# Transfers of two images at a time, edges cleared one by one and two filtered pairs in the second convolution of an attention and quantised-convolution kernel

## The chip, the core and the metric

The kernel runs on one core of a Trainium2 chip. The core has five engines that work side by side, each through its own instructions in order: TensorE (PE in the profile, its weight loads PEld), VectorE (DVE), ScalarE (ACT), GpSimd (POOL) and SyncE (SP), which here only issues transfers (DMAs). The transfers are carried out by 16 DMA engines. SBUF, the memory next to the engines, has 128 partitions; DRAM holds the inputs, the output and two intermediate arrays. The metric is the device time of one execution in microseconds (us), the median of several runs.

## What is computed

An input of 16 images with 128 channels of 32 x 32 pixels goes through two layers. The first is attention with four heads over the 1024 pixels of each image, with a residual; the second is two 3 x 3 convolutions on 4-bit activations with 4-bit weights, each followed by a batch norm over all images, with a second residual:

```python
x = out + x                                  # layer 0: attention, its output projection, residual
identity = x
out = act_quant(x)                           # clip to 0..1, round to 15 levels
out = conv3x3(out, weight_quant(w1))
out = batchnorm(out, gamma1, beta1)          # mean and variance over images and pixels
out = act_quant(out)
out = conv3x3(out, weight_quant(w2))
out = batchnorm(out, gamma2, beta2)
return out + identity
```

## The kernel before

A first phase, some 1900 of the 2013 us, does the attention and, image by image, the first convolution. It leaves two arrays in DRAM: `x1d`, the 16 x 128 x 1024 array that is the second residual (`identity`), and `y1d`, the first convolution's output for 15 of the 16 images. The last image's part of this is the end of the phase (`normalise_group`, lines 880 to 890, with `quantize` at 253 to 266, and `first_conv` at 1002).

The change lies in the last phase, lines 1149 to 1342. It does the second convolution. The images are taken in eight pairs (p = 0 to 7, images 2p and 2p + 1), and the 128 output channels in two halves (`COLS`, "part" 0 and 1). One convolution of one pair for one half fills 128 partitions of a PSUM tile: 64 channels of the first image in the upper 64 partitions, 64 of the second in the lower ones (`HALVES`). So the phase runs over all eight pairs for part 0, and then over all eight for part 1:

- Four transfers (line 1179) bring `y1d` back, 2, 3, 4 and 6 images at a time, with the channels on the partitions. They are issued by SP.
- Each image has a padded tile of 34 x 34 pixels in bf16 (`pads2`), whose edges are zero. Three such tiles are left over from the phase before; the edges of the other 13 are cleared by 26 memsets on POOL (lines 1185 and 1186) as the phase begins.
- `quantize2` (1195 to 1206) turns one image into 4-bit steps: one activation on ACT (the first, 1200, is on DVE), and two operations on DVE (1203 and 1206), the last of which writes the inside of the padded tile.
- `pair_conv` (1235 to 1251) is the direct convolution of 16 rows of a pair: 9 taps x 2 images = 18 matmuls of 64 output channels over 512 pixels; a pair takes 36. `filtered_conv` (1253 to 1274) does the same for a whole pair with four filtered combinations of rows: 4 x 3 x 2 = 24 matmuls, and then five operations on ACT and DVE to combine them. It needs `rows`, four combinations of the rows of each image, which `transform2` (1210 to 1216) makes with four POOL operations per image. Only part 1 uses it, for the pairs in `FILTERED`: 1, 3 and 5. The rows for pairs 1 and 3 are asked for during part 0 (1323 to 1326), those for pair 5 during part 1 (1332 to 1335).
- Statistics of each convolution (`bn_stats`, line 1287 and 1250) go into the batch norm of the half; `parameters` (1306) makes its scale and bias when all eight pairs are done.
- `finish` (1291 to 1304) scales a pair's result on ACT, adds the residual on DVE (1301) and stores it. The residual comes from `load_residual` (1190 to 1193). Both the load and the store of a pair are two transfers, one for each image: 64 partitions, 256 KB. The residuals of part 0 are loaded as soon as the phase begins; part 0 is finished pair by pair during part 1, and each finished pair is followed by the load of the same pair's residual for part 1, into the same buffer. Part 1 is finished after its own statistics, at the very end; the first three pairs' stores are cut in smaller pieces there (`parts`, 1340).

The order of instructions on each engine is fixed when the kernel is built. SP's transfers of this phase are, in order: the loads of `y1d` (with the store of the last image of `x1d` between the first and the second of them), the residuals of part 0, then store and load in turn for the eight pairs, then the stores of part 1.

The two sides of a transfer are described by access patterns: a list of counts and steps, the slowest first. For the residual of one image it is 64 channels x 1024 values on the DRAM side and 64 partitions x 1024 values in SBUF. For `y1d` the pattern is turned so that 128 channels come first on the DRAM side as well ("b c n -> c b n").

Of the kernel before, what the change touches and what calls it, by code (L numbers as in the profile page):

```python
# [10 lines left out]
BF16 = mybir.dt.bfloat16  # L11
AF = mybir.ActivationFunctionType
ALU = mybir.AluOpType
# [180 lines left out]
def fast_path(  # L194
# [17 lines left out]
    P = 128  # L212
    B, C, N = x.shape
# [4 lines left out]
    W = 32  # L218
    H = N // W
    NTAP = 9  # L220
    RPH = HALF // W
    NPAD = 3
# [25 lines left out]
    for i in range(NPAD):  # L248
        t = padp.tile([P, H + 2, W + 2], BF16, name=f"pad{i}")
# [59 lines left out]
    STEP = 128.0  # L309
# [67 lines left out]
    with ExitStack() as ph:  # L377
# [57 lines left out]
        for hf in range(NHF):  # L435
            for i, queue in enumerate((nc.sync, nc.scalar)):
                half = (ts(i, P // 2), ts(hf, HALF))
# [625 lines left out]
        for g in range(LAST):  # L1063
            b, h = heads[g]
# [44 lines left out]
        for step in range(n_steps):  # L1109
            g, k = divmod(step, NK)  # L1110
# [38 lines left out]
    with ExitStack() as ph:  # L1149
# [3 lines left out]
        padf = pool("padf", 1)  # L1153
# [11 lines left out]
        LAST_PAIR = B // 2 - 1  # L1165
        COLS = (slice(0, P // 2), slice(P // 2, P))
        HALVES = (slice(0, P // 2), slice(P // 2, P))
        FILTERED = (1, 3, 5)

        def prepare(behind):  # L1170
            with tc.issue_after(behind):
# [9 lines left out]
                ys[AWAY.start + i] = back[:, i - lo]  # L1181
        pads2 = list(pads)
        for b in range(NPAD, B):
            t = padf.tile([P, H + 2, W + 2], BF16, name=f"padf{b}")
            nc.gpsimd.memset(t[:, 0 : H + 2 : H + 1, :], 0.0)
            nc.gpsimd.memset(t[:, 1 : H + 1, 0 : W + 2 : W + 1], 0.0)
            pads2.append(t)
        x1 = {}

        def load_residual(part, p):  # L1190
            t = x1[part, p] = resp.tile([P, N], F32, tag=f"res{p}", name=f"res_{part}_{p}")
            for i, half in enumerate(HALVES):
                nc.sync.dma_start(out=t[half], in_=x1d[2 * p + i, COLS[part]])  # L1193

        def quantize2(b, r0=0, r1=H):

            t = steps.tile([P, (r1 - r0) * W], BF16, tag="steps", name="steps")
            y = ys[b][:, r0 * W : r1 * W]
            if (b, r0) == (0, 0):
                nc.vector.tensor_scalar(t, y, scale1, bias1, ALU.mult, ALU.add)  # L1200
            else:
                nc.scalar.activation(t, y, AF.Identity, bias=bias1, scale=scale1)  # L1202
            nc.vector.tensor_scalar(t, t, STEP, STEP + A_LEVELS, ALU.max, ALU.min)  # L1203
            into = pads2[b][:, r0 + 1 : r1 + 1, 1 : W + 1]
            t = t.rearrange("p (h w) -> p h w", w=W)
            return nc.vector.tensor_scalar(into, t, STEP, None, ALU.subtract)

        rows = {}

        def transform2(b):  # L1210
            rows[b] = rowp.tile([P, 4, D, W + 2], BF16, tag="rows", name=f"rows2_{b}")
            pick = lambda r: pads2[b][:, r : r + 2 * D - 1 : 2, :]
            four = ((0, 2, ALU.subtract), (1, 2, ALU.add), (2, 1, ALU.subtract), (1, 3, ALU.subtract))
            for k in (1, 2, 0, 3):
                x, y, op = four[k]
                nc.gpsimd.tensor_tensor(rows[b][:, k], pick(x), pick(y), op)

        def place2(part, p, i):
            if p < LAST_PAIR:
# [33 lines left out]
        def filtered_conv(part, p):  # L1253
            m = [None] * 4
            for k in (1, 2, 0, 3):
                m[k] = ps_c.tile([P, D, W], F32, tag="c", name=f"psf{part}_{p}_{k}")
                for dx in range(3):
                    for i, half in enumerate(HALVES):
                        nc.tensor.matmul(
                            m[k][half],  # L1260
                            lhsT=weights[k][:, dx, COLS[part]],
                            rhs=rows[2 * p + i][:, k, :, dx : dx + W],
                            start=(dx == 0),
                            stop=(dx == 2),
                        )
            y = ys[2 * p + part].rearrange("p (i r w) -> p r i w", r=2, w=W)
            new = lambda what: sump.tile([P, D, W], F32, tag=what, name=f"{what}_{p}")

            half, total = new("half"), new("total")
            nc.scalar.mul(half, m[1], 0.5)  # L1270
            nc.vector.scalar_tensor_tensor(total, m[2], 0.5, half, ALU.mult, ALU.add)
            nc.vector.tensor_tensor(y[:, 0], m[0], total, ALU.add)
            nc.vector.scalar_tensor_tensor(half, m[2], -0.5, half, ALU.mult, ALU.add)
            nc.vector.tensor_tensor(y[:, 1], half, m[3], ALU.subtract)
# [3 lines left out]
        def convolve(part, p):  # L1278
            if part and p in FILTERED:
                filtered_conv(part, p)  # L1280
            else:
                ends = starts.get(p if p or not part else None, (0, RPH, H))
                for i, (r0, r1) in enumerate(zip(ends, ends[1:])):
                    pair_conv(part, p, r0, r1 - r0, i if p == LAST_PAIR else None)
            if p < LAST_PAIR:
                for hf in range(NHF):
                    nc.vector.bn_stats(place2(part, p, hf), ys[2 * p + part][:, ts(hf, HALF)])  # L1287
            if p == LAST_PAIR - 1:
                gather2(part)

        def finish(part, p, scale, bias, ends=(0, N)):
            y = ys[2 * p + part]
            for lo, hi in zip(ends, ends[1:]):
                some = y[:, lo:hi]
                if part and p == 0 and hi <= N // 2:
                    nc.vector.tensor_scalar(some, some, scale, bias, ALU.mult, ALU.add)
                elif len(ends) > 2 and p == 0:
                    nc.scalar.activation(some, some, AF.Identity, bias=bias, scale=scale)
                elif lo == 0:
                    nc.scalar.activation(y, y, AF.Identity, bias=bias, scale=scale)  # L1300
                added = nc.vector.tensor_tensor(some, some, x1[part, p][:, lo:hi], ALU.add)  # L1301
                for i, half in enumerate(HALVES):
                    nc.sync.dma_start(out=out[2 * p + i, COLS[part], lo:hi], in_=some[half])  # L1303
            return added

        def parameters(part):
            swap(part, 6, 6 + 3 * STATS, 3 * STATS)
            return bn_params(1, late2[part], gb2[part])

        for r0, r1 in ((0, 10), (10, RPH + 2), (RPH + 2, H)):  # L1310
            for b in range(2):
                first = quantize2(b, r0, r1)
        for b in (2, 3):
            quantize2(b)
        prepare(first.ins)
        for p in range(B // 2):
            load_residual(0, p)
        for p in range(B // 2):
            convolve(0, p)
            for b in (2 * p + 4, 2 * p + 5):  # L1320
                if b < B:
                    quantize2(b)
            for f in FILTERED[:2]:
                if p == f + 1:
                    transform2(2 * f)
                    transform2(2 * f + 1)
        scale2, bias2 = parameters(0)
        for p in range(B // 2):
            convolve(1, p)
            added = finish(0, p, scale2, bias2)  # L1330
            load_residual(1, p)
            for f, g in zip(FILTERED, FILTERED[2:]):
                if p == f:
                    transform2(2 * g)
                    transform2(2 * g + 1)
            if p == 4:
                with tc.issue_after(added.ins):
                    nc.vector.tensor_copy(flag, worst[0:1, :])
        scale2, bias2 = parameters(1)
        parts = {0: (0, N // 4, N // 2, N), 1: (0, N // 2, N), 2: (0, N // 2, N)}  # L1340
        for p in range(B // 2):
            finish(1, p, scale2, bias2, parts.get(p, (0, N)))
# [108 lines left out]
def attention_then_quantized_convs(  # L1451
# [50 lines left out]
    def conv_weights(n, wp, behind):  # L1502
# [19 lines left out]

    flag = const.tile([1, 1], mybir.dt.int32, name="flag")
    fast_path(
        nc, tc, x, xturned, wqk, wvo, bo, bnp, x1d, y1d, out, bo_sb, bnp_sb, quad, wq, sc, flag, conv_weights,
        constants,
# [85 lines left out]
```

## Time and profile before

| | |
|---|---|
| three runs | 2015.11, 2015.13, 2016.14 us, median 2015.13 |
| the profiled execution | 2015.25 us in all, of which the span from first to last instruction is 2013.4 us |
| mean granted TensorE clock | 0.993 |
| PE busy | 1972.8 us, 98% of the span |
| DVE busy | 1542.4 us, 77% |
| ACT busy | 1174.2 us, 58% |
| POOL busy | 201.3 us, 10% |

The last phase in stretches, in us from the start of the span:

| stretch | what happens | PE busy | DVE busy | granted clock | GB/s |
|---|---|---|---|---|---|
| 1903.0 to 1907.0 | last image, memsets | 2.31 of 4.00 | 3.76 | 1.00 | 233 |
| 1913.5 to 1925.8 | part 0, pairs 0 and 1 | 9.30 of 12.30 | 9.57 | 1.00 | 409 |
| 1925.8 to 1930.0 | part 0, pair 2 | 4.16 of 4.20 | 4.13 | 0.59 | 280 |
| 1930.0 to 1938.0 | part 0, pairs 2 and 3 | 5.59 of 8.00 | 7.55 | 1.00 | 230 |
| 1938.0 to 1954.0 | part 0, pairs 4 to 7 | 16.00 of 16.00 | 12.27 | 1.00 | 115 |
| 1957.0 to 1973.0 | part 1, to pair 5 | 16.00 of 16.00 | 15.29 | 1.00 | 228 |
| 1973.0 to 1989.5 | part 1, to its scale and bias | 8.88 of 16.50 | 15.92 | 0.93 | 293 |
| 1989.5 to 2001.0 | part 1 finished | 0 | 10.18 | 0.50 | 137 |
| 2001.0 to 2013.4 | last stores | 0 | 0 | 0.50 | 215 |

Such a row adds up, for one stretch, what each engine was busy with; the GB/s are what the 16 DMA engines moved in it. A stretch in which PE is busy throughout is set by PE; one in which it is idle is set by what PE waits for.

### The profile page before, as it was taken

The numbers are of one execution on the slowest core, as the hardware profiler recorded it, in microseconds if no ns is written. First come the engines' busy times: TensorE is split into PE (matmuls) and PEld (weight loads), VectorE is DVE, ScalarE is ACT, GpSimd is POOL, SyncE is SP. The second block draws the span as 40 slices with busy tenths as digits, with TensorE's granted clock in tenths as the row PEclk, the third lists the DMA queues.
The fourth block names the chain that finished last, engine by engine and source line by source line (L and its number), as shares of the span: only waits on it lengthen the run. The fifth ranks groups of instructions, "written<-read, shape, count | busy, mean of one in ns | idle before, by whom it ended". The sixth has DMA issues, their size and how long they took to land.

```text
span 2013.4 us, 26882 instructions
## 1 busy us (share of the span) xinstructions
PE 1972.8 (98%) x10021; PEld 993.9 (49%) x10021; DVE 1542.4 (77%) x2713; ACT 1174.2 (58%) x2024; POOL 201.3 (10%) x257
## 2 busy tenths in 40 slices
PE   9999999999999999999999999999999999999983
PEld 4455544545454454545445454554545445455552
DVE  5886869778686977868697786878768687877887
ACT  4556556565655656565565656556555655656463
POOL 1110010001001010000101000100000010000041
PEclk9999999999999999999999999999999999999997
DMA  4343333433343333334343343433334343342278
GB/s 122 85 90 88 95 74 96 93 84 95 91 98 72 96 90 88 95 84 105 66 102 84 87 103 83 97 73 101 89 84 100 78 101 79 95 89 67 76 215 241
DMA packets 56747, 193.85 MB, mean 96 GB/s; under 512 B 6944, under 2 KB 7328, under 8 KB 56608
## 3 DMA queue, kind: packets, MB, share of 16 engines
q0 software_dynamic: 27216, 99.10, 25.9%
q1 hardware_dynamic: 26272, 83.18, 11.9%
q10 hardware_dynamic: 3120, 9.77, 1.5%
q8 instruction: 80, 1.31, 0.3%
q14 instruction: 59, 0.48, 0.1%
HBM read 35.27 MB, written 24.64 MB: 30 GB/s over the span
## 4 chain that ended last, share of the span: by engine, by line
PE 96%; DVE 2%; ACT 1%; DMA 0%; issue 0%; SPq 0%; DVEq 0%; ACTq 0%
PE pss L412 44%; PE psa L412 38%; PE psu L412 5%; PE pso L412 5%; PE psw L412 2%; PE psd L1241 1%; ACT steps L1202 0%; SPq L1303 0%; DVE early L1287 0%; DVE back L1301 0%; DMA res<-x_dram 0%; DMA x<-in_x_dram 0%; SPq L1193 0%; PE psv L412 0%; DVE steps L1203 0%
## 5 line engine op out<-in xcount | busy, mean ns | idle before, releaser
L412 PE MATMUL pss<-u,x 128*64 128x512 f32 (+1 forms) x4128 | 1032.5, 589 | 0.0
L412 PE MATMUL psa<-e,xt 128*64 128x512 f32 x3472 | 897.9, 592 | 0.0
L594 ACT ACTIVATE e<-pss 128x512 f32<-128x512 f32 x1008 | 590.8, 597 | 442.2 <-PE pss L412 435.9
L412 PEld LDWEIGHTS pss<-u,x 128*64 128x64 f32 x4128 | 437.7, 137 | 436.0 <-issue 400.1
L412 PEld LDWEIGHTS psa<-e,xt 128*64 128x64 f32 x3472 | 379.1, 137 | 371.9 <-issue 351.3
L579 DVE TENSOR_TENSOR e<-e 128x512 f32<-128x512 f32 x252 | 172.0, 682 | 299.6 <-ACT e L594 299.2
L604 POOL DMA_DIRECT2D es<-e x189 | 163.1, 863 | 1679.3 <-DVE e L583 1383.7
L580 DVE TENSOR_TENSOR e<-e 128x1024 f32<-128x1024 f32 x252 | 307.7, 1221 | 10.3 <-ACT e L594 8.6
L412 PE MATMUL psu<-x,at_sb 128*64 128x512 f32 x512 | 183.4, 592 | 0.2 <-DMA x<-in_x_dram 0.2
L583 DVE TENSOR_TENSOR e<-e 128x512 f32<-128x512 f32 x252 | 173.1, 687 | 10.9 <-DVE e L580 0.5
L634 ACT COPY ev<-psa 128x512 f32<-128x512 f32 x189 | 99.2, 593 | 63.1 <-PE psa L412 61.7
L412 PE MATMUL pso<-z,wb_sb 128*64 128x512 f32 (+1 forms) x480 | 132.3, 539 | 0.0
L543 ACT ACTIVATE u<-psu,au_sb 128x512 f32<-128x512 f32 x127 | 87.3, 687 | 8.3 <-PE psu L412 5.6
L412 PEld LDWEIGHTS psu<-x,at_sb 128*64 128x64 f32 x512 | 61.3, 137 | 55.8 <-issue 54.6
L670 DVE TRANSPOSE_TENSOR_REDUCE part<-es 128x32 f32<-128x1024 f32 (+1 forms) x65 | 79.5, 1223 | 9.9 <-DMA es<-e 9.9
L710 DVE STREAM_TRANSPOSE rb<-sums 128x1024 f32<-128x1024 f32 (+1 forms) x66 | 79.9, 1210 | 1.6
L730 DVE TENSOR_TENSOR z<-av,rb 128x512 f32<-128x512 f32 x120 | 78.3, 685 | 0.0
L412 PEld LDWEIGHTS pso<-z,wb_sb 128*64 128x64 f32 x480 | 53.0, 137 | 44.6 <-issue 40.9
L801 DVE TENSOR_TENSOR y<-sa,s 64x512 f32<-64x512 f32 x15 | 10.2, 683 | 66.4 <-ACT sa L785 66.4
L660 ACT COPY ev<-y 64x512 f32<-64x512 f32 x63 | 38.8, 616 | 33.1 <-DVE y L657 31.8
L412 PE MATMUL psw<-rows,filters 128*64 128x256 bf16 x540 | 57.5, 277 | 0.0
L412 PEld LDWEIGHTS <-filters 128*64 128x64 bf16 x540 | 44.8, 109 | 24.0 <-issue 18.5
(205 smaller groups left out, 1405.7 us busy)
## 6 DMA issues: line engine op xcount, KB each, us to landing
es<-e POOLq DMA_DIRECT2D x189, 512.0 KB, 4.5
es<-e SPq DMA_DIRECT2D x63, 512.0 KB, 2.9
xt<-in_xturned_dram SPq DMA_DIRECT2D x32, 256.0 KB, 3.0
x_dram<-acc SPq DMA_DIRECT2D x16, 512.0 KB, 2.9
res<-x_dram SPq DMA_DIRECT2D x32, 256.0 KB, 6.5
x<-in_x_dram ACTq DMA_DIRECT2D x15, 512.0 KB, 4.2
y_dram<-y SPq DMA_DIRECT2D x15, 512.0 KB, 2.6
out_dram<-back SPq DMA_DIRECT2D x24, 256.0 KB, 4.3
```

The costliest lines, as they stand in the source:

```text
L412: done = nc.tensor.matmul(out_, lhsT=lhsT, rhs=rhs, start=start, stop=stop)
L543: copied = nc.scalar.activation(dst, ps, AF.Identity, bias=au_sb[:, h : h + 1])
L579: nc.vector.tensor_tensor(e[:, T3], e[:, B12], e[:, B22], ALU.add)
L580: nc.vector.tensor_tensor(e[:, T1 : T2 + 1 : T2 - T1], e[:, B12 : B11 + 1], e[:, B11 : T3 + 1 : T3 - B11], ALU.subtract)
L583: return nc.vector.tensor_tensor(e[:, T4], e[:, T2], e[:, B21], ALU.add)
L594: exps[:] = [nc.scalar.activation(e[:, 2 * c + 1 - m], ps, AF.Exp).ins]
L604: nc.gpsimd.dma_start(out=sides[g], in_=mine, accum_op=ALU.add)
L634: nc.scalar.copy(evs[g][i], psa[g][i])
L660: nc.scalar.copy(sa[BOTTOM], y[BOTTOM])
L670: nc.vector.tensor_reduce(part, total.rearrange("p (k c) -> p k c", c=Q), AX.X, ALU.add, apply_transpose=True,)
L710: nc.vector.transpose(rb, rinv.unsqueeze(2).to_broadcast([P, n, Q]))
L730: nc.vector.tensor_tensor(z[:, 2 * (h % 2) + 1 - m], av[:, ts(m, HALF)], rb[:, ts(m, HALF)], ALU.mult)
```

## The change

- Residual loads and stores take both images of a pair in one transfer: the SBUF side is all 128 partitions of the tile, the DRAM side two images x 64 channels x 1024 values (or the piece that is stored).
- The 26 memsets no longer stand at the head of the phase. `clear(b + 3)` follows the last operation of `quantize2(b)`, so the edges of one image are cleared after each of the first 13 quantised images.
- Two pairs are filtered, 2 and 5, in place of 1, 3 and 5; their rows are all asked for after part 0's loop and put behind the last quantisation.

```diff
-        FILTERED = (1, 3, 5)
+        FILTERED = (2, 5)
...
         for b in range(NPAD, B):
-            t = padf.tile([P, H + 2, W + 2], BF16, name=f"padf{b}")
-            nc.gpsimd.memset(t[:, 0 : H + 2 : H + 1, :], 0.0)
-            nc.gpsimd.memset(t[:, 1 : H + 1, 0 : W + 2 : W + 1], 0.0)
-            pads2.append(t)
+            pads2.append(padf.tile([P, H + 2, W + 2], BF16, name=f"padf{b}"))
+
+        def clear(b, behind):
+            with tc.issue_after(behind):
+                nc.gpsimd.memset(pads2[b][:, 0 : H + 2 : H + 1, :], 0.0)
+                nc.gpsimd.memset(pads2[b][:, 1 : H + 1, 0 : W + 2 : W + 1], 0.0)
+
...
-            for i, half in enumerate(HALVES):
-                nc.sync.dma_start(out=t[half], in_=x1d[2 * p + i, COLS[part]])
+            nc.sync.dma_start(out=t, in_=x1d[2 * p : 2 * p + 2, COLS[part]])
...
-            return nc.vector.tensor_scalar(into, t, STEP, None, ALU.subtract)
+            done = nc.vector.tensor_scalar(into, t, STEP, None, ALU.subtract)
+            if r1 == H and b + NPAD < B:
+                clear(b + NPAD, done.ins)
+            return done
...
-        def transform2(b):
+        def transform2(b, behind):
...
-                nc.gpsimd.tensor_tensor(rows[b][:, k], pick(x), pick(y), op)
+                with tc.issue_after(behind):
+                    nc.gpsimd.tensor_tensor(rows[b][:, k], pick(x), pick(y), op)
...
-                for i, half in enumerate(HALVES):
-                    nc.sync.dma_start(out=out[2 * p + i, COLS[part], lo:hi], in_=some[half])
+                nc.sync.dma_start(out=out[2 * p : 2 * p + 2, COLS[part], lo:hi], in_=some)
...
             for b in (2 * p + 4, 2 * p + 5):
                 if b < B:
-                    quantize2(b)
-            for f in FILTERED[:2]:
-                if p == f + 1:
-                    transform2(2 * f)
-                    transform2(2 * f + 1)
+                    last = quantize2(b)
+        for f in FILTERED:
+            for b in (2 * f, 2 * f + 1):
+                transform2(b, last.ins)
...
-            for f, g in zip(FILTERED, FILTERED[2:]):
-                if p == f:
-                    transform2(2 * g)
-                    transform2(2 * g + 1)
```

## The prediction, made before the changed kernel ran

> **What bounds the kernel now.** I read the chain of waits over the last 150 us first, then the stage sums, the transfers stretch by stretch, and the instructions in order of time. The attention phase is PE from end to end and the change leaves it alone, so only the last 110 us count. The chain there:
>
> ```profile
> by line: PE psd L1241 18.4%; PE psa L412 12.6%; PE pss L412 11.4%; issue 6.0%; ACT steps L1202 3.6%; SPq L1303 3.2%; DVE early L1287 2.6%; DVE back L1301 2.6%; DMA res<-x_dram 2.5%; SPq L1193 2.3%; DVE steps L1203 1.9%; DVE padf L1206 1.9%;
> ```
>
> The direct convolution leads, and the quantisation (L1202, L1203, L1206) and the residual's transfers and stores follow. From the instructions in order of time:
>
> ```profile
> 1904.06 2.33 DVE L261 TENSOR_SCALAR qt<-qt 128x256 f32<-128x256 f32 x1
> 1904.13 0.24 POOL L1185 MEMSET padf<- 128x68 bf16 x1
> ...
> 1920.62 0.43 DVE L1206 TENSOR_SCALAR padf<-steps 128x1024 bf16<-128x1024 bf16 x1
> ...
> 1925.46 14.74 POOL L1216 TENSOR_TENSOR rows<-padf 128x544 bf16<-128x544 bf16 x12
> ...
> 1927.05 1.22 DVE L1206 TENSOR_SCALAR padf<-steps 128x1024 bf16<-128x1024 bf16 x1
> ```
>
> A DVE operation beside the 26 memsets takes 2.33 us, where its like takes 0.29 at 1907.61; a quantising operation takes 0.43 us alone and 1.22 beside POOL's rows. So POOL holds up DVE, DVE holds up PE. What PE then lost, in the list of waits and in the stage sums:
>
> ```profile
> PE psd L1241 <- DVE padf L1206: 5.1, 3, 2.4
> ```
>
> ```profile
> 1925.80:1930.00 4.20, 4.16 (x24) 1.86 (x26) 4.13 (x5) 2.14 (x3) 4.20 (x4) 0.59 1.06 280
> ```
>
> That is 5.1 us of idleness in three waits, and after the first long wait a stretch of 4.2 us at a granted clock of 0.59, which costs another 4.2 x 0.41 = 1.7 us.
>
> Now the transfers: all of q1 between 1913 and 1926 (`y1d` coming back, 128 partitions), then between 1927 and 1945 (residuals, 64 partitions), then the issues by size.
>
> ```profile
> DMA packets 1337, 5.36 MB, mean 412 GB/s; under 512 B 32, under 2 KB 32, under 8 KB 1336
> q1 hardware_dynamic: 1336, 5.34, 102.0%
> ...
> DMA packets 1253, 4.13 MB, mean 230 GB/s; under 512 B 250, under 2 KB 250, under 8 KB 1249
> q1 hardware_dynamic: 1249, 4.09, 102.5%
> ```
>
> ```profile
> res<-x_dram SPq DMA_DIRECT2D x32, 256.0 KB, 6.5
> out_dram<-back SPq DMA_DIRECT2D x24, 256.0 KB, 4.3
> ```
>
> Both stretches keep all 16 engines busy (102%) with packets of about 4 KB; the first moves 412 GB/s, 25.75 for each engine, the second 230. So the shape of a transfer, not its bytes, sets its rate.
>
> **The change, part by part.**
>
> The transfers. The DRAM side of each new one is two images x 64 channels x 1024 values: its slowest count is 2. Every transfer in the list of issues has 64 or 128 as its slowest count on both sides (`y1d` was turned to get 128), and those keep 16 engines busy. No row shows a slowest count of 2. What has to be priced is how such a transfer is shared out. The SBUF side can be cut anywhere with one step from partition to partition; the DRAM side cannot, because between the 64th channel of one image and the first of the next it jumps over the other half. Equal shares that follow the slowest count of both sides are two: image 0 on one engine, image 1 on another. The bounds: 16 engines at the best row, 412 GB/s; two engines at that row's rate for each, 2 x 25.75 = 51.5 GB/s. I take the two engines. The nearest row in how the sides are laid out is that of the halves, which shows that a smaller slowest count went with a lower rate (128: 412, 64: 230); nothing shows that sharing can look past the slowest count.
>
> Bytes: 32 residual loads x 256 KB are 8.39 MB; the stores are the same array's size, 8.39 MB. On two engines 16.78 MB / 51.5 GB/s = 325.8 us. They run in one queue behind `y1d`, whose transfers end at about 1927.2 (the rate falls from over 400 to 230 there). SP's order has nothing else to offer in between: residuals of part 0, store and load in turn, stores of part 1. The loads of part 0 alone take 16 x 5.1 = 81 us, until 2007; by then part 0 is convolved and scaled, so stores are ready when their turn comes. DVE's add for pair 7 waits until 2007 plus a landing, and behind it, in DVE's order, the statistics of the last pairs of part 1 and its scale and bias: part 1's results are ready by some 2020. Its last residual lands after 24/32 of the bytes, at about 2170, and then the stores take 81 us more. Nothing of this waits for an engine: transfers set the end.
>
> The memsets go from the head of the phase to 13 places of two, 0.24 us from one to the next now, each behind a quantised image. L261 falls from 2.33 to 0.30: -2.0 us. The chain through it (L886, then SP's store of `x1d`, behind which SP holds the other `y1d` loads; SP waits 4.1 us there) moves up as much, and so do the transfers: `y1d` ends at 1925.2. The memsets' new places cost DVE at most 13 x 0.25 = 3.3 us, hidden here under the transfers.
>
> The rows. 20 of 24 POOL operations (1.30 us mean) stood beside quantisations or beside part 1; now 16 stand behind the last quantisation. DVE's 0.43 us comes back, PE's 5.1 + 1.7 us can be won. One pair goes from 24 matmuls to 36: 1964.09 - 1960.12 = 3.97 us for pair 2 against 2.64 for pair 1, +1.3 on PE, and four DVE operations of 0.67 us fewer, -2.7. Under 325 us of transfers all of it is hidden, and worth nothing; without that cover it is the sum of the second rival.
>
> The sum, in the profiled execution's time: 1925.2 + 325.8 = 2251.0; from the last transferred byte (about 2011.0) to the end of the span there are 2.4 us now, so 2253.4; outside the span 2015.25 - 2013.4 = 1.85, so **2255 us**. The profiled execution lies 0.1 above the median of 2015.13, which changes nothing.
>
> Its bounds: slices of the 412 GB/s stretch run from 378 to 466; at 466 the transfers take 288 us and the time is 2218. If loads run at the rate of 64 partitions on each engine (230 / 16 = 14.4 GB/s), they take 292 instead of 163 us: 2384. That rate came with 16 engines writing into 64 partitions, where here two write; so I go halfway, to 2320.
>
> [...] The rows of 412 and 230 say that halves do cost something here; no row shows a slowest count of 2.
>
> **The rivals.**
>
> 1. Only loads are confined. A store's source is SBUF, slowest count 128; if sharing followed the source alone, stores would stay on 16 engines. Then 8.39 MB / 51.5 = 163 us of loads, and 8.39 MB / 412 = 20 us of stores in the same queue: 1925.2 + 183 + 2.4 + 1.85 = 2113. For it: stores and loads behave differently already (the mixed stretch 1960 to 1985 moves 295 GB/s, just what loads at 230 and stores at 412 give in equal parts). Against: both sides have to be cut alike.
>
> 2. On the other side: transfers spread over 16 engines, as the partitions of the tile do. Then the change does what its parts say. Memsets -2.0. Of the 5.1 us of PE waits some 3.5 go (image 9 and its like still have to arrive), with the low clock's 1.7: -5.2. Part 1 ends on DVE today (PE's last matmul about 1982, last statistic 1987.05), so the filtered pair given up is worth 2.7 on DVE and its 1.3 on PE fits into the slack: -2.7. Rows for pair 5 are ready 16 x 1.3 = 21 us after the last quantisation, about when PE asks. At the end 22 + 2 stores, 0.75 us apart, spread over 18 us (1990.66 to 2008.78); 12 stores of 0.33 us (the issue of `x_dram<-acc`, 128 partitions) and 10.2 us of bytes at 412 keep up with DVE, whose last add ends 10.2 us after the scale and bias: that end comes at about 10.2 + 0.3 + 1.3 + 2.4 = 14.2 us in place of 23.9, -9.7. Together -19.6: 1996. Between 1989 and 2003 by its parts. It decides from the point where a transfer is shared among some 14 or more engines: 16.78 MB in the 88 us between `y1d` and today's end are 191 GB/s, 7.4 engines, and the stores of the end need more.
>
> **How the numbers follow.** Two engines 0.86, loads alone confined 0.04, sixteen engines 0.09, anything else 0.01. The predicted time is the likeliest case's. Its own bounds 2215 to 2320 hold about 0.93 of it, so 0.80 in all: this is the range, and neither rival is in it. A difference under 0.2% (4 us) can't be told from no change. Faster is rival 2: 0.09. Slower is the first case and rival 1: 0.90. No difference needs a chance balance: 0.01.
>
> **What would show it.** Right: in the last slices the DMA share falls to about 2 of 16 engines at some 51 GB/s, for over 300 us; residual loads of 512 KB take tens of us to land; the chain of waits ends in transfers; PE is idle for the last 250 us; L261 takes 0.3 us; quantising operations take 0.43 us throughout, and yet none of that shows in the time. Wrong: a stretch of residual loads at 230 GB/s or more, and 12 stores at the end landing within 5 us each. If the share is at two engines but the rate isn't 51, the size is off and not the mechanism; a share of 4 or 8 sixteenths would mean another rule of sharing.

## The result, and the profile after

The changed kernel takes 2256.72 us, the median of 6 runs (2256.23 to 2257.34), against 2015.13 us before on the same chip (6 runs, 2014.61 to 2016.14): 1.1198 times as long, with a 95% interval of 1.1184 to 1.1213. The prediction was 2255. The profiled execution has 2257.22 us, its span 2255.3.

From the page of the changed kernel, first the span cut into 40 slices of 56.4 us (the granted clock in tenths, the DMA engines' busy share in tenths, and what they moved), then the chain that ended last, by engine:

```profile
PE   9999999999999999999999999999999999920000
...
PEclk9999999999999999999999999999999999965555
DMA  4343334343334333434343333434343423311111
GB/s 118 81 89 94 85 94 94 81 98 84 94 84 94 87 92 75 112 66 108 73 105 80 94 86 96 91 85 94 87 100 76 94 71 99 121 53 52 52 52 49
...
PE 84%; DMA 8%; SPq 4%; DVE 0%; issue 0%; POOL 0%; DVEq 0%; POOLq 0%
```

Up to the 33rd slice this is the attention phase, which the change leaves alone. In the last five the DMA engines are busy to one tenth and move 49 to 53 GB/s, and in the last four PE does nothing. The transfers of the last phase, from 1930 to 2250 us, by queue (packets, MB, share of 16 engines):

```profile
DMA packets 4653, 16.77 MB, mean 52 GB/s; under 512 B 70, under 2 KB 326, under 8 KB 4639
...
q1 hardware_dynamic: 4639, 16.62, 12.8%
```

12.8% of 16 engines are 2.05 engines, and the packets are as large as before (4 KB), so each of the two moves 52 / 2 = 26 GB/s, about what each of the 16 moved in the stretch of 412 GB/s before. The chain of waits from 1927 us to the end, by line, with some of its pieces (start, length, what):

```profile
by line: DMA res<-x_dram 53.3%; SPq L1195 12.3%; SPq L1308 7.2%; DVE back L1307 1.2%; issue 0.6%; DVE y L1307 0.4%; DVE back L1278 0.2%; DVE half L1279 0.2%; DVEq L1307 0.0%
...
1997.37 34.11 DMA res<-x_dram
...
2038.15 33.85 DMA res<-x_dram
```

A residual load is some 34 us on the way, where one of half the size took 6.5 before. No work of PE is left in the chain, which the direct convolution led before, and DVE's adds have under 2% of it. In the list of waits (us in total, times, longest), DVE waits for residuals, and PE for the padded tiles of part 0, as before:

```profile
DVE back L1307 <- DMA res<-x_dram: 157.7, 12, 19.2
...
PE psd L1247 <- DVE padf L1208: 4.6, 5, 1.7
```

The second line is the first sign that something else did not happen. In order of time (start, length, engine):

```profile
1903.79 0.15 POOL L1188 MEMSET padf<- 128x68 bf16 x1 [35.83 <-PE psa L412]
...
1904.86 2.34 DVE L261 TENSOR_SCALAR qt<-qt 128x256 f32<-128x256 f32 x1
...
1906.74 0.31 POOL L1189 MEMSET padf<- 128x64 bf16 x1
...
1923.49 9.89 POOL L1222 TENSOR_TENSOR rows<-padf 128x544 bf16<-128x544 bf16 x8 [11.54 <-issue]
...
1929.92 1.21 DVE L1208 TENSOR_SCALAR padf<-steps 128x1024 bf16<-128x1024 bf16 x1
```

All 26 memsets run in one go from 1903.79 us, at the head of the phase, and L261 between them still takes 2.34 us. The rows of pair 2 run at 1923.49, beside the quantisation, and a quantising operation beside them still takes 1.21 us. `issue_after` named an instruction of DVE, and POOL did not wait for it: neither move took place. The stages (PE, PEld, DVE, ACT and POOL busy, the granted clock, DMA share, GB/s) show how little that mattered here:

```profile
1930.00:1950.00 20.00, 17.14 (x149) 8.45 (x148) 19.20 (x25) 12.36 (x15) 13.28 (x11) 1.00 0.13 53
2100.00:2170.00 70.00, 0.00 (x0) 0.00 (x0) 3.68 (x3) 0.00 (x0) 0.00 (x0) 0.50 0.13 52
```

While PE and DVE were busy, the transfers crept along at the same 53 GB/s as later (52), when nothing else but three additions ran.

### The profile page after: what moved, and what is told of

Its sections match the earlier page's. It is cut to its first block, busy times and chain, and to the rows that moved or that the text cites. A ratio compares the mean times of both kernels' runs of the same rounds, so it can differ in the third digit from the quotient of the medians.

```text
span 2255.3 us, 26852 instructions
## 1 busy us (share of the span) xinstructions
PE 1978.7 (88%) x10032; PEld 990.5 (44%) x10033; DVE 1541.4 (68%) x2709; ACT 1174.4 (52%) x2025; POOL 191.3 (8%) x249
## 4 chain that ended last, share of the span: by engine, by line
PE 84%; DMA 8%; SPq 4%; DVE 0%; issue 0%; POOL 0%; DVEq 0%; POOLq 0%
PE pss L412 39%; PE psa L412 34%; DMA res<-x_dram 8%; PE psu L412 5%; PE pso L412 4%; SPq L1195 2%; PE psw L412 2%; SPq L1308 1%; PE unread L412 0%; DVE back L1307 0%; PE psv L412 0%; DVE qt L261 0%; PE ps_a L412 0%; SPq L1179 0%; PE psr L412 0%
## 5 line engine op out<-in xcount | busy, mean ns | idle before, releaser
L1307 DVE TENSOR_TENSOR back<-back,res 128x1024 f32<-128x1024 f32 (+2 forms) x19 | 18.6, 998 | 158.4 <-DMA res<-x_dram 157.7
L1247 PE MATMUL psd<-padf,wq 128*64 128x512 bf16 (+1 forms) x432 | 51.9, 377 | 11.2 <-DVE back L1280 6.1
```

What stands on the lines that cost most here:

```text
L1247: nc.tensor.matmul(ps[half], lhsT=wq[1][:, tap, COLS[part]], rhs=pads2[2 * p + i][:, r0 + dy : r0 + dy + n_rows, dx : dx + W], start=(tap ...
```

## The experiments

Times are medians, and each ratio is against the kernel before, run on the same chip in turn with it. "In halves" means two transfers of 64 partitions, one for each image, as the kernel before has them.

### The transfers alone

The kernel before, with nothing but the two-image loads and stores:

```diff
-            for i, half in enumerate(HALVES):
-                nc.sync.dma_start(out=t[half], in_=x1d[2 * p + i, COLS[part]])
+            nc.sync.dma_start(out=t, in_=x1d[2 * p : 2 * p + 2, COLS[part]])
...
-                for i, half in enumerate(HALVES):
-                    nc.sync.dma_start(out=out[2 * p + i, COLS[part], lo:hi], in_=some[half])
+                nc.sync.dma_start(out=out[2 * p : 2 * p + 2, COLS[part], lo:hi], in_=some)
```

> The kernel before with nothing but the two-image loads and stores. Theory: transfers set the end and the other edits are covered, so the same time as the changed kernel: 1927.2 + 325 + 3 + 1.9 = 2257, 2252 to 2262. Rival (a part of the 240 us comes from the filtered pairs, the rows or the edges): clearly below, by what these cost.

Measured: 2256.84 us, ratio 1.1197 (1.1164 to 1.1229), the same as the whole change. All of the loss is in the transfers, and the other parts are worth nothing under them.

### Loads in halves, or stores in halves

The changed kernel with one of the two loops of the diff above put back.

> The changed kernel with the residual loads back in two transfers of 64 partitions; the stores keep both images in one. Theory (slowest count of 2, two engines, stores as well as loads): part 0's stores can begin at about 1958, one is ready every 4 us and takes 10.2 us, so they and the loads behind them in the queue run without a break: 16 x 10.2 = 163 us of stores, and 32 loads x 4 packets x 0.16 to 0.29 us = 20 to 37 us on the same two engines; 1958 + 163 + 28 + 3 + 1.9 = 2154, 2140 to 2170, with a DMA share near 2 of 16 in the stores. Rival (only loads are confined, stores follow their 128-partition source): 2000 to 2015.

> The changed kernel with the stores back in two transfers of 64 partitions; the loads keep both images in one. Theory: 16 loads x 10.2 us = 163 us on two engines from the end of y1d at 1927.7, with 16 stores of part 0 between them that put 4 packets of 0.16 us on each engine, 10 us: the last residual lands at about 2101, its pair's add and store follow, 2101 + 1.2 + 1.2 + 4 + 1.9 = 2109, 2100 to 2125. With the run that halves the loads the two delays add up to about that of the change (240 us), as one queue carries both. Rival (only stores confined): about 2013.

Measured: with loads in halves 2142.61 us, ratio 1.063 (1.0599 to 1.0661); with stores in halves 2121.9, ratio 1.0527 (1.0497 to 1.0558). The queue's line in the stretch where only stores move (2060 to 2119 us, loads in halves), and in a stretch of loads (1930 to 1980 us, stores in halves):

```profile
q1 hardware_dynamic: 1155, 3.07, 13.0%
```

```profile
q1 hardware_dynamic: 635, 2.56, 12.7%
```

Both have two engines' share, 13.0 x 16 / 100 = 2.08 and 2.03, at 52 GB/s. So a store, whose SBUF side counts 128, is confined by its DRAM side just as a load is, and the first rival, that only loads are, falls: it would have had 2113 us for the whole change, and the run with loads in halves not slower than before. The two losses, 126.9 and 106.2 us, make 233 of the 241.6 that both cost together; they add up nearly, as two parts of one queue's work would.

### The rest alone

The changed kernel with both in halves: memsets, rows and the two filtered pairs without the transfers that hid them.

> The changed kernel with both loads and stores back in halves, so only the edges, the rows and the two filtered pairs differ from before. Theory (from the changed kernel's trace: the 26 memsets still run in one go at 1903.8 and L261 still takes 2.34 us; the rows still stand beside quantisations, from 1923.5 and from 1938.2; the marks don't hold POOL back): the edits of order do nothing, only the filtered pair given up counts, 2.7 us less on DVE: 2010 to 2016, L261 at 2.3 us. Rival (the edits do what the change says): -2.0 - 5.2 - 2.7, so 2005, and L261 at 0.3 us.

Measured: 2013.14 us, ratio 0.9989 (0.998 to 0.9998). In order of time it shows the memsets in one go again and L261 with them:

```profile
1904.16 2.33 DVE L261 TENSOR_SCALAR qt<-qt 128x256 f32<-128x256 f32 x1
...
1937.65 9.90 POOL L1223 TENSOR_TENSOR rows<-padf 128x544 bf16<-128x544 bf16 x8 [6.06 <-DVE padf L1209]
```

What is left of the second rival here is one filtered pair less, for which it had 2.7 us; the run lies 2.4 us under the kernel before (2015.53). No run gave up the pair by itself: this one also filters pair 2 in place of pairs 1 and 3 and makes the rows at other times, so that the 2.4 us are the pair's is argued, not shown.

### What decides how many engines

If the slowest count of the DRAM side sets the number of engines, then other counts must give other numbers. Part 0's residual loads, 512 KB and 128 partitions each, were given four DRAM sides, with all else as in the run before; then the same with the counts in the order 16, 8, 4, 2, so that the fast ones do not run into what the slow ones leave behind:

```diff
-            for i, half in enumerate(HALVES):
-                nc.sync.dma_start(out=t[half], in_=x1d[2 * p + i, COLS[part]])
+            if part:
+                for i, half in enumerate(HALVES):
+                    nc.sync.dma_start(out=t[half], in_=x1d[2 * p + i, COLS[part]])
+            else:
+                n = (2, 4, 8, 16)[p // 2]
+                nc.sync.dma_start(out=t, in_=x1d[0:n, 0 : P // n])
```

> Both halved again, except the eight residual loads of part 0, which each bring 128 rows of 4 KB in one transfer, from 2 images x 64 channels (pairs 0 and 1), 4 x 32 (2 and 3), 8 x 16 (4 and 5) and 16 x 8 (6 and 7). They read other images' channels, so part 0's residual isn't the reference's. Theory (the engines are as many as the slowest count): 51, 103, 206 and 412 GB/s, a DMA share of 2, 4, 8 and 16 sixteenths, 10.2, 5.1, 2.5 and 1.3 us for each transfer; all eight have landed 38 us after y1d, near 1966, and the whole time is near that of before, 2010 to 2018. Rival (any pattern that jumps between images is carried by two engines, or at a fixed rate): 51 GB/s throughout, the eighth lands 82 us after y1d, near 2010, and the whole time is 2025 or more.

> [...] Part 0's residual is read from other images' channels. Theory: four clean steps from y1d's end on, 412 GB/s for 2.5 us, 206 for 5, 103 for 10 and 51 for 20. Rival (fixed rate for any pattern that jumps between images): one level from end to end.

Measured: 2019.21 and 2019.09 us, one execution each, beside 2015.75 and 2015.53 of the kernel before; the first is just above the 2010 to 2018 that were expected. In the first run the steps of 2 and 4 stand clear (52 and 90 GB/s), while 8 and 16 run into each other. The second run, in four stretches from 1928, 1932, 1940 and 1952 us, for counts of 16, 8, 4 and 2:

```profile
DMA packets 210, 0.76 MB, mean 253 GB/s; under 512 B 25, under 2 KB 25, under 8 KB 210
...
q1 hardware_dynamic: 210, 0.76, 102.8%
...
DMA packets 230, 0.89 MB, mean 128 GB/s; under 512 B 13, under 2 KB 13, under 8 KB 229
...
q1 hardware_dynamic: 229, 0.88, 56.5%
...
DMA packets 255, 1.03 MB, mean 94 GB/s; under 512 B 8, under 2 KB 8, under 8 KB 252
...
q1 hardware_dynamic: 252, 1.00, 25.1%
...
DMA packets 95, 0.39 MB, mean 56 GB/s; under 512 B 2, under 2 KB 2, under 8 KB 94
...
q1 hardware_dynamic: 94, 0.38, 13.3%
```

The shares of 16 engines are 102.8, 56.5, 25.1 and 13.3%: 16, 9, 4 and 2 engines. The stretch of 8 has a little of its neighbour in it. So the number of engines follows the count of images, and the step that the prediction took without a row for it is shown. The rates, though, are not four times the same thing: with 2 and 4 engines some 26 and 23 GB/s for each, with 16 only 253 / 16 = 15.8. Two runs asked why.

In the first, otherwise the run with counts of 16, 8, 4 and 2, each image of `x1d` stands 129 channels from the next, so that the 16 reads of a load no longer lie 512 KB apart:

```diff
-                nc.sync.dma_start(out=x1d[b], in_=acc)
+                nc.sync.dma_start(out=x1d[b, 0:P], in_=acc)
...
-    args.append(nc.dram_tensor("x1_dram", (b, c, h * w), F32, kind="Internal").ap())
+    args.append(nc.dram_tensor("x1_dram", (b, c + 1, h * w), F32, kind="Internal").ap())
```

In the second, part 0's loads with a slowest count of 64 write the middle of the tile instead of a half of it, and loads of 32 rows fill the rest:

```diff
-            for i, half in enumerate(HALVES):
-                nc.sync.dma_start(out=t[half], in_=x1d[2 * p + i, COLS[part]])
+            if part:
+                for i, half in enumerate(HALVES):
+                    nc.sync.dma_start(out=t[half], in_=x1d[2 * p + i, COLS[part]])
...
+        for p in range(B // 2):
+            nc.sync.dma_start(out=x1[0, p][32:96], in_=x1d[2 * p, COLS[0]])
+        for p in range(B // 2):
+            nc.sync.dma_start(out=x1[0, p][0:32], in_=x1d[2 * p + 1, 0:32])
+            nc.sync.dma_start(out=x1[0, p][96:128], in_=x1d[2 * p + 1, 32:64])
```

> As the run with the DRAM-led counts 16, 8, 4, 2 of part 0's residual loads, but each image of x1d stands 129 channels from the next instead of 128, one of them unused, so that image starts are 528,384 bytes apart instead of 524,288. In that run counts 16, 8, 4, 2 moved 253, 128, 94 and 56 GB/s, and a load led by 128 rows moved 408 with the same 16 engines, each writing 8 partitions. Theory A (the DRAM addresses: 16 reads at a step of 512 KB meet in the same place): with the step broken, count 16 goes to about 400 GB/s and count 8 to about 200, with DMA shares still near 102% and 50%. [...] The time is 2016 to 2022 us under both. Part 0's residuals of the loads are read from other images and channels, as in that run.

> The changed kernel with loads and stores in halves, but part 0's residuals are loaded in another shape: first, for all eight pairs, 64 channels of one image into partitions 32 to 95 (2.1 MB), then for all eight pairs twice 32 channels into partitions 0 to 31 and 96 to 127 (2.1 MB). Halves into partitions 0 to 63 or 64 to 127 moved 230 GB/s at a DMA share of 102%. [...] Rival (a slowest count of 64 costs that by itself, wherever it is written): the first 2.1 MB move at 230 GB/s too and take 9.1 us. The time is 2010 to 2018 us under both. Part 0's residuals stand in other partitions than they belong to.

Measured: the other spacing does not help. Counts of 16 and 8 move 238 and 133 GB/s with the images apart (2019.69 us, one execution, beside 2016.96 before); from 1928 to 1931 us, with a count of 16:

```profile
DMA packets 192, 0.71 MB, mean 238 GB/s; under 512 B 18, under 2 KB 18, under 8 KB 192
```

Where in the tile a load writes does count (2013.26 us, one execution, beside the same 2016.96). The loads into the middle, from 1926 to 1932 us, with the end of `y1d` at their head (from 1927.7 to 1931.7 us alone the rate is 407 too):

```profile
DMA packets 722, 2.44 MB, mean 407 GB/s; under 512 B 129, under 2 KB 129, under 8 KB 721
...
q1 hardware_dynamic: 721, 2.43, 101.6%
```

A slowest count of 64 moves 407 GB/s when it is written to partitions 32 to 95, and 230 when it is written to 0 to 63 and 64 to 127 in turn; the engines are busy in both (101.6 and 102.5%). So here the rate depends on the partitions that are written. The loads of 32 rows behind them moved 196 GB/s from 1933 to 1943 us at a share of 74%, with gaps between them. What makes the partitions count no run shows, and why counts of 8 and 16 are slow stays open too.

### The two moves, really made

To make POOL wait, the operations were given something to wait for in the data. The edges of image b + 3 are written as 0 times a part of image b's quantised tile, and the rows stand behind a copy, on POOL, of a column of the last quantised image:

```diff
-        def clear(b, behind):
-            with tc.issue_after(behind):
-                nc.gpsimd.memset(pads2[b][:, 0 : H + 2 : H + 1, :], 0.0)
-                nc.gpsimd.memset(pads2[b][:, 1 : H + 1, 0 : W + 2 : W + 1], 0.0)
+        def clear(b, done):
+            nc.gpsimd.tensor_scalar(
+                pads2[b][:, 0 : H + 2 : H + 1, :], done[:, 1:3, :], 0.0, None, ALU.mult
+            )
...
+        behind = nc.gpsimd.tensor_copy(seen, pads2[B - 1][:, H, W : W + 1])
         for f in FILTERED:
             for b in (2 * f, 2 * f + 1):
-                transform2(b, last.ins)
+                transform2(b, behind.ins)
```

> As the run with only the rest, but with POOL really held back: the edges of image b + 3 are written as 0 times values of image b's quantised tile, so they wait for it, and the rows stand on POOL behind a copy of one value of the last quantised image. Theory (POOL beside DVE is what delays part 0): L261 takes 0.3 us, quantising operations 0.43 us but for short meetings with the edges, PE's waits for the padded tiles in part 0 shrink from 5.1 to some 1.5 us; -2.0 - 3.5 - 1.7 against the run with only the rest, 2003 to 2009. Rival (the waits are for y1d's transfers, or the rows come too late for pair 2 in part 1): within 2 us of that run, or slower.

Measured: 2014.25 us, ratio 0.9992 (0.9983 to 1.0001): no gain over the rest alone, and the expectation is missed. From the order of time and the list of waits:

```profile
1904.63 0.25 DVE L261 TENSOR_SCALAR qt<-qt 128x256 f32<-128x256 f32 x1
...
1945.30 19.17 POOL L1227 TENSOR_TENSOR rows<-padf 128x544 bf16<-128x544 bf16 x16
```

```profile
PE psd L1252 <- POOL padf L1190: 3.6, 1, 3.6
```

```profile
1920.00:1924.00 4.00, 2.94 (x16) 1.83 (x17) 0.00 (x0) 0.00 (x0) 3.62 (x10) 0.66 1.02 411
```

Both moves are there now: L261 takes 0.25 us in place of 2.33, and all 16 row operations stand behind the quantisation. But the edges of image 3, the first that needs them, now come late: POOL begins with them at 1920.11, though the last operation on image 0, which they stand behind, ended at 1913.80 (why POOL waited longer than that was not taken apart). PE waits 3.6 us for them and then runs a stretch at a granted clock of 0.66 (1920 to 1924 us). That wait takes the place of the one removed.

So the edges of the first three images went back to the head of the phase, six memsets in place of 26, and the others wait as in the run before:

```diff
         for b in range(NPAD, B):
-            pads2.append(padf.tile([P, H + 2, W + 2], BF16, name=f"padf{b}"))
+            t = padf.tile([P, H + 2, W + 2], BF16, name=f"padf{b}")
+            if b < 2 * NPAD:
+                nc.gpsimd.memset(t[:, 0 : H + 2 : H + 1, :], 0.0)
+                nc.gpsimd.memset(t[:, 1 : H + 1, 0 : W + 2 : W + 1], 0.0)
+            pads2.append(t)
...
-            if r1 == H and b + NPAD < B:
+            if r1 == H and NPAD <= b and b + NPAD < B:
```

> The run with the true order, except that the edges of images 3, 4 and 5 are memset at the head of the phase (6 memsets, about 0.7 us), so that no early pair waits for them. Theory: in the true order PE lost 3.6 us to POOL's late edges of image 3 and 3.4 us at half clock after it (1.7 us); without these 5.3 us the order is worth what the second rival gave it: 2014.3 - 5.3 = 2009, 2006 to 2011. Rival (what part 0 gains is lost again in part 1, where the rows now stand beside DVE's adds): 2012 to 2015.

Measured: 2009.97 us, ratio 0.9974 (0.9963 to 0.9984), 5.1 us under the kernel before on the same chip and far under the changed one. L261 takes 0.25 us here too. PE waits 2.6 us for padded tiles in place of 5.1 before, and from 1907 to 1927 and from 1928 to 1938 us it has a granted clock of 1.00, where before it was 0.59 from 1925.8 to 1930. In the stage of pairs 4 to 7 of part 0 PE is busy throughout, as before the change, which in the run of the rest alone it is not. That stage of the two, this one first:

```profile
1938.00:1954.00 16.00, 16.00 (x166) 10.32 (x164) 12.41 (x27) 6.20 (x11) 13.03 (x14) 1.00 0.44 101
```

```profile
1938.00:1954.00 16.00, 14.60 (x149) 8.37 (x145) 15.32 (x23) 8.36 (x12) 9.55 (x8) 1.00 0.49 117
```

### One transfer of 128 rows, and a second queue

If the number of engines follows the slowest count, a load of both images is fast when its 128 rows follow each other in DRAM. `x1d` was laid out by pair and half; its stores become two of 64 partitions each:

```diff
-                nc.sync.dma_start(out=x1d[b], in_=acc)
+                for part in range(2):
+                    nc.sync.dma_start(
+                        out=x1d[b // 2, part, ts(b % 2, P // 2)], in_=acc[ts(part, P // 2)]
+                    )
...
-            for i, half in enumerate(HALVES):
-                nc.sync.dma_start(out=t[half], in_=x1d[2 * p + i, COLS[part]])
+            nc.sync.dma_start(out=t, in_=x1d[p, part])
```

> The run with only the rest, but with the intermediate array x1 laid out by pair and channel half, so that the two images' 128 rows of a residual load lie one behind the other: one load of 128 partitions whose slowest count is 128 on both sides (each store of x1 becomes two, of 64 partitions). Theory: the same 512 KB in one transfer moves at about 410 GB/s and part 0's residuals have all landed some 10 us after y1d, near 1938 in place of 1945; the time stays that of the run with only the rest, 2010 to 2015, as the loads are hidden. Rival (one transfer for 128 partitions is slow whatever its pattern): 51 GB/s, and 2100 or more; or 230 GB/s as for halves.

Measured: the loads move 408 GB/s, as expected of them, and the time is 2014.32 us, ratio 0.9996 (0.9987 to 1.0005). The queue's lines from 1928 to 1938 us:

```profile
DMA packets 1102, 4.08 MB, mean 408 GB/s; under 512 B 108, under 2 KB 108, under 8 KB 1101
...
q1 hardware_dynamic: 1101, 4.07, 102.0%
```

This is the load that the change was after, at eight times its rate, and it is not worth anything: other work covers the residuals at 230 GB/s already. (The new layout has a price of its own: the last image's store of `x1d`, issued ahead of `y1d`'s loads, is two issues in place of one, and PE waits 3.3 us for the first padded tiles, where the rest alone has 0.7.)

At the end the stores are issued one after the other on SP, 24 in 18 us. The last run took the order mended and the new layout, and gave the second image's stores of part 1 to POOL's queue:

```diff
                 for i, half in enumerate(HALVES):
-                    nc.sync.dma_start(out=out[2 * p + i, COLS[part], lo:hi], in_=some[half])
+                    queue = nc.gpsimd if part and i else nc.sync
+                    queue.dma_start(out=out[2 * p + i, COLS[part], lo:hi], in_=some[half])
```

> The mended order and the relaid loads together, and in part 1's stores the second image of each pair is issued by POOL in place of SP. Theory: the last 24 stores are bound by SP's issues (0.75 us each over 18 us, while DVE's last add ends 10 us after the scale and bias); with two queues the end follows DVE and the bytes (4.19 MB at 412 GB/s, 10.2 us): 6 to 7 us less than the mended order, so 2000 to 2005, faster than both kernels. Rival (the stores are bound by their transfers, or POOL issues late beside DVE's adds): within 2 us of the mended order.

Measured: 2012.76 us, ratio 0.999 (0.9981 to 0.9999): missed, and slower than with the order mended alone (2009.97 on the same chip). The last issues, in order of time, and two stretches behind them (the granted clock, DMA share and GB/s at the end):

```profile
1997.50 0.54 POOL L1324 DMA_DIRECT2D out_dram<-y  x1 [0.60 <-DVE y L1321]
1998.34 1.74 SPq L1324 DMA_DIRECT2D out_dram<-y  x1
...
2000.00:2003.00 3.00, 0.00 (x0) 0.00 (x0) 0.00 (x0) 0.00 (x0) 0.00 (x0) 0.50 1.00 328
2004.00:2009.50 5.50, 0.00 (x0) 0.00 (x0) 0.00 (x0) 0.00 (x0) 0.00 (x0) 0.50 0.00 0
```

The scale and bias are made at 1986.74 us, so the last issue ends 13.3 us behind them, where with the order mended alone it ends 19.2 us behind (2003.51 against 1984.30). But the span ends 9.4 us after the last issue in place of 4.6, and the scale and bias come 2.4 us later. Issuing was shortened by 5.9 us, and the end came 1.4 us later in the profile. The trace shows three things that the theory had left out. The 2.4 us seem to come with the new layout, which this run took over as well: from 1913.5 to 1925.8 us PE is busy for 8.22 of 12.30 us, where the order mended alone has 10.67. With the issues out of the way the DMA engines themselves are full (a share of 1.00 from 2000 to 2003 us): from 1992 to 2002 us they move 316 GB/s, where 412 were reckoned with. And the bytes are all moved by 2004.0 us, after which nothing runs for 5.5 us until the span ends; with the order mended the bytes end at 2005.8, with 2.3 us left. What holds the end back for these 5.5 us is open.

## Why the prediction was right, and where it was not

**Two engines.** Right, and shown: the share is 12.8% of 16, the numbers of engines follow the DRAM side's slowest count through 16, 8, 4 and 2 (102.8, 56.5, 25.1 and 13.3%), and loads and stores are confined alike (12.7 and 13.0%). That such a transfer runs on two was the author's estimate from how its two sides can be cut, with no row behind it when it was made. The price was taken from the 412 GB/s row, 51.5 for two engines; the profile has 52. From 1927.7, where the rate falls, to the last byte at about 2252.3 (the end of the thirty-second of 40 slices of 2240 to 2255.3 us) the transfers take 324.6 us; the prediction had 325.8. On the way there, part 1's scale and bias are made at 2023.3 (the prediction had some 2020) and its last residual lands at 2172.0 (about 2170). Joining two halves cost 241 us where the joined DRAM side begins with 2, and gave the better rate where its 128 rows follow each other (408 GB/s in place of 230, at a share of 102.0%). The bound with slow loads, 14.4 GB/s for each engine, did not come: sixteen engines had that rate when they wrote into one half of the partitions, and 407 / 16 = 25.4 when they wrote into the middle 64; two engines kept 52 / 2 = 26.

**The rest of the sum.** The start was put at 1925.2 and was 1927.7; the tail after the last byte at 2.4 and was 3.0. Of the first error 2.0 have a cause: the sum took 2.0 us off for the memsets, and they did not move. The rest goes with the whole phase, which began 0.8 us later in this profile (its first transfer was issued at 1903.81 in place of 1903.01). With -1.2 for the transfers, +2.5 for the start, +0.6 for the tail and +0.1 for what lies outside the span (1.92 in place of 1.85) the profiled 2257.2 is 2.0 above the 2255.2 that the terms add up to.

**The step that failed.** The prediction read the change as moving the memsets to thirteen places and the rows behind the last quantisation, and expected L261 at 0.3 us and quantising operations at 0.43 throughout. None of this came: the memsets ran in one go from 1903.79, L261 took 2.34, the rows ran from 1923.49 and quantising operations beside them took 1.2. An order asked for behind an instruction of another engine did not hold POOL back; data to wait for did (the rows ran from 1945.30). It did not matter for the time only because the transfers covered everything else. That the change might not do what it says was worth a rival here, and the trace of before could not have told.

**What the cover hid.** The terms of the second rival, which had 1996 us, were looked at without the transfers. One filtered pair less had -2.7; the rest alone, in which only that term is left, gave -2.4 us (-4.0 to -0.4 by the interval of its ratio). Memsets and rows really moved had -2.0 and -5.2; the best order, with the first three images' edges left in front, lies 5.1 us under the kernel before on its chip and the rest alone 2.4 on its own, so they gave some 2.7. The rival had overlooked that clearing behind a quantisation can itself be late: 3.6 us of PE and a stretch at a granted clock of 0.66. From the scale and bias of part 1 to the end the span has 24.1 us before (1989.27 to 2013.4), 24.5 with the rest alone (from 1985.32) and 23.8 with the order mended: no part of the change but the stores bears on it, and -9.7 for twelve stores of 16 engines could not be seen, since transfers of that shape got two. Its bytes were priced at 412 GB/s, a rate read off loads; the last stores in halves moved 316 with two queues and full engines. The second queue, which shortens the issuing by other means, did not bring it.

**The first rival** falls by the run with the loads in halves: the stores alone cost 127 us.

## What to carry to other kernels

Read a transfer's DRAM side before joining two: here a joined pattern that begins with a count of 2 ran on two engines at 52 GB/s, where the halves had 230, and 128 partitions on the SBUF side did not help; the share of the DMA engines in the trace (12.8% of 16) shows it at once. Lay the array out so that the long count comes first, but only where the transfer is on the path: here the same load at 408 GB/s gained nothing (a ratio of 0.9996 to before). An order between two engines exists where the trace shows the later one waiting, not where it is written down: here POOL's rows ran from 1923.49 us, while the quantisation went on past 1948.

## What the runs showed of the hardware that was not expected

- Busy engines are not fast engines. Shares of 102 to 103% went with 407, 253 and 230 GB/s, the first and the last by which partitions were written; what sets the 253 is open. Loads into partitions 32 to 95 were 1.8 times as fast as loads into a half.
- With a DRAM side led by 16 images, 16 engines moved 253 GB/s, with 8 images 128, with 4 images 94; 128 rows in a row moved 408. Another spacing of the images in DRAM did not help (238 and 133 GB/s for 16 and 8).
- After a 3.6 us wait of PE the granted clock was 0.66 over four microseconds (1920 to 1924 us), so the wait cost more than its length; before the change it was 0.59 from 1925.8 to 1930 us.
- With half of the last stores on POOL's queue the span ended 9.4 us after the last issue and 5.5 us after the last byte; with all on SP's, 4.6 and 2.3 us.
